# Cross products of one expert with kept first halves and early hub products, and a shared expert block's output products spread over six units

## The chip, the cores and the metric

The kernel runs on one core of one Trainium2 chip. The time is device microseconds of one execution. Before the change it is 2487.79 us, the median of 3 runs (2487.12 to 2488.73).

The core has a matrix engine (PE), two elementwise engines (DVE and POOL), an engine for activations and copies (ACT), and a queue that issues transfers (SP). Each works through its own list of instructions in order and waits for the others by semaphores.

## The reference

A gated layer with 8 weighted experts and one shared expert, added to its input. In float32, for 8 sequences of 512 tokens of width 256, with 1024 hidden features per expert:

```python
g = einsum('bsd,edf->ebsf', h, Wg)
u = einsum('bsd,edf->ebsf', h, Wu)
expert_outs = einsum('ebsf,efd->ebsd', silu(g) * u, Wd)
expert_output = einsum('be,ebsd->bsd', gating_probs, expert_outs)
shared = einsum('bsf,fd->bsd', silu(h @ Sg) * (h @ Su), Sd)
return x + (1 - sg) * expert_output + sg * shared
```

## The kernel before

**Units.** The work is cut into units: 2 groups of 4 sequences, times 9 experts (the shared one is the ninth), times 2 groups of 4 blocks of 128 features. A unit takes 4 blocks of weights and 4 sequences, and makes the 16 gate and 16 up products of blocks with sequences. The width of 256 is two halves of 128.

**Fewer products.** Block i and sequence i are given a small constant each. The four products of equal index, the *hub*, are made in two halves: P_i from the first half (`P_step`, L697) and then Q_i on top (`Q_step`, L724). The twelve others come in six pairs (i, j): one product of differences (`R1_step`, L785), started from the seed f = P_j - P_i, serves both (i, j) and (j, i). Each of these then gets one product more (`R_step`, L802) and a correction by the hub results D. Thus a pair costs 3 products in place of 4, for gate and for up.

**Banks.** The results lie in PSUM banks: three for gate, three for up, and two (`po0`, `po1`) for the output products. A seed is copied into a bank by ACT (L784), DVE opens the second bank of the pair (L798) and adds D (L811), ACT takes silu (L681), DVE multiplies (L686). POOL makes weight operands u and wb (L606, L622, L623) and the sums `rows` and `cols` of the features (L848).

**Output products.** `down` makes 26 products of a unit with Wd, again in pairs (r, S or s, r) and with the sums (p with `rows`, q with `cols`). They begin in the second half of their unit, 15 of them there and 11 in the next, mixed into the gate and up products.

**One expert in eight blocks.** Expert 7 is handled with all 8 blocks and all 8 sequences at once. Its units have kinds. A (unit 14) makes blocks 0 to 3 with sequences 0 to 3. X (unit 15) makes the 16 cross pairs (i, n), i below 4, n from 4 to 7, with four more hub products n (`hub_P`, `hub_Q`). Z (unit 33) makes blocks 4 to 7 with sequences 4 to 7. L (unit 32) has only output products, since X left its features in DRAM; they run as a *guest*, in the last unit before Z and in Z itself (`guest_down`).

**Seeds of X.** For pair (i, n) the difference P_n - P_i is taken by `hub_difference` (L775): for gate on DVE, for up on POOL. P_i is loaded from DRAM for each pair anew (`load_P`), into the tile that then takes the difference.

**What sets the order.** Strings of letters: G takes the next step of gate and up, D the next output product, E the next step of the guest. PE and POOL follow the written order; DVE and ACT are ordered by the framework's scheduler, but for operations that are pinned. With each D from the second on, `step_ahead` also takes one step of making operands for later units: transposed inputs, and for each pair a difference, a scaling and two sums, which go to DRAM (`xs`, `xsX`, `xsZ`) and come back when wanted.

Of the kernel before, what the change touches and what calls it, by code (L numbers as in the profile page):

```python
# [16 lines left out]
def kernel(  # L17
# [52 lines left out]
    CO = tuple(c - 0.5 for c in CI)  # L70
    ACROSS = [(i, NI + j) for j in range(NI) for i in range(NI)]
# [232 lines left out]
    def prepare(h):  # L304

        for p, (i, j) in enumerate(PAIRS):
# [10 lines left out]
            gp.tensor_tensor(v, v, at[j][:, 0], ALU.subtract)  # L317
            yield
            if d != 1.0:
                gp.tensor_scalar(v, v, 1.0 / d, 0.0, ALU.mult, ALU.add)  # L320
                yield
            gp.tensor_tensor(B_j, v, B_j, ALU.add)
# [12 lines left out]
    def prepare_across():  # L335

        for q, (i, n) in enumerate(ACROSS):
            to = dram.tile([P, 3, S], F32, tag=f"xsX_{q}", name=f"xsX_{q}")
            if i == 0:
# [5 lines left out]
            f = form_tile()  # L345
            pin(ve.tensor_sub(f[:, 0], xhub[0, i][:, 0], hub[:, 0]))
            yield
            pin(ve.tensor_scalar(
                f[:, 0], f[:, 0], 1.0 / (CI[i] - CO[n - NI]), 0.0, ALU.mult, ALU.add
            ))  # L350
            yield
            yield
            pin(ve.tensor_add(f[:, 1], f[:, 0], hub[:, 1]))
            yield
# [12 lines left out]
    def prepare_inner():  # L367

        for p, (i, j) in enumerate(PAIRS):
# [12 lines left out]
            if d != 1.0:  # L382
                pin(ve.tensor_scalar(v, v, 1.0 / d, 0.0, ALU.mult, ALU.add))
                yield
# [133 lines left out]
    for h in range(NH):  # L518
        for e in range(NE):
            for g in range(GRP):  # L520
# [16 lines left out]
                u.ca, u.opened, u.xo, u.a2 = {}, {}, {}, None  # L537
# [3 lines left out]
    for u in units:  # L541
        u.nxt = next((v for v in units[u.n + 1 :] if v.kind != "L"), None)
        u.guest = units[u.n + 1] if u.nxt and u.nxt.kind == "Z" else None
        if u.kind != "N":
            u.oct = octets.setdefault(u.e, {})

# [34 lines left out]
    def make_at(u, i):  # L581
# [5 lines left out]
        if u.C[i] % 1.0 and i not in u.ca:  # L587
            scaled_w(u, i)
# [152 lines left out]
    def hub_P(u, n, m):  # L741

        bank = u.bank[n, n, m] = new_bank(u, m, f"c{n}{n}")
        nc.tensor.matmul(bank, u.raw[n][:, m, 0], u.xo[n][:, 0], start=True, stop=True)
        t = u.Ps[n, m] = zpool.tile([P, S], F32, tag="z", name=f"P{n}{m}_{u.name}")
        nc.scalar.copy(t, bank)
        store_half(u, ("P", n), m, t)

# [17 lines left out]
    def load_P(u, p):  # L766

        for m in range(2):
            t = ppool.tile([P, S], F32, tag="p", name=f"f{p}{m}_{u.name}")
            nc.sync.dma_start(t, u.oct["P", u.pairs[p][0]][:, m])  # L770
            u.f[p, m] = t

    def hub_difference(u, p, m):

        (gp if m else ve).tensor_tensor(  # L775
            u.f[p, m], u.Ps[u.pairs[p][1], m], u.f[p, m], ALU.subtract
        )
# [101 lines left out]

    def load_kept(u, what, pool, tag):  # L880
# [4 lines left out]
    def look_ahead(u, items):  # L885

        if u.kind not in "XL":
            return
        for k, what in enumerate(items):
            if isinstance(what, str):  # L890
                which = "rows" if what[0] == "p" else "cols"
                n, sums = int(what[1]), getattr(u, which)
                if u.kind == "L" and n not in sums:
                    sums[n] = load_kept(u, (which, n), sumpool, "sum")
                continue
            for i, j in (PAIRS[what], PAIRS[what][::-1]):
                if u.kind == "L" and (i, j) not in u.h_:
                    u.h_[i, j] = load_kept(u, ("h", i, NI + j), hpool, "h")
            if k < (2 if u.kind == "X" else 1) and what not in u.X:
# [3 lines left out]
    def down(u, acc):  # L903
# [102 lines left out]
        if u.kind == "X":  # L1006
            order = DOWN_ACROSS
        elif u.n + 1 < len(units):
# [4 lines left out]
        for k, what in enumerate(order):  # L1013
            look_ahead(u, order[k : k + 3])
            if isinstance(what, int):
                yield from pair(what)
# [177 lines left out]
    def prepare_next(u, p):  # L1194

        nxt = u.nxt
        if nxt.kind == "X":
# [15 lines left out]
            if p >= 4:  # L1213
                load_P(nxt, p - 4)
# [7 lines left out]
        if p == 4 and nxt.guest:  # L1222
            load_d(nxt.guest, iopool, "io")

    def end_next(u, p):

        nxt = u.nxt
        if nxt.kind == "X":
# [3 lines left out]
            if p == 5:  # L1232
                for m in range(2):
                    hub_difference(nxt, 0, m)
                seed(nxt, 0)
                for m in range(2):
                    hub_difference(nxt, 1, m)

    def first_step(u, m):

        nxt = u.nxt
        if nxt.kind == "X":
            hub_P(nxt, NI, m)
        elif nxt.kind == "Z":
# [10 lines left out]
    FORMS_AT = {6: 0, 7: 1, 8: 3, 9: 2, 10: 4, 13: 5}  # L1255

    def across(u):
# [5 lines left out]
        last = len(u.pairs) - 1  # L1263
        for q, (i, n) in enumerate(u.pairs):
            if i == 0:
                for m in range(2):
                    hub_Q(u, n, m)
                    yield
                    R1_step(u, q, m)
                    yield  # L1270
            if i == 0 and n + 1 < 2 * NI:
# [3 lines left out]
            if q + 2 <= last:  # L1275
                load_P(u, q + 2)
            if i == 1 and n + 1 < 2 * NI:
                hub_load(u, n + 1)
            if i == 3 and n + 2 < 2 * NI:
                load_w(u, n + 2)  # L1280
            if q >= last - 3:
                prepare_next(u, q - last + 5)
            if q < last and i < NI - 1:
# [5 lines left out]
            for m in range(2):  # L1289
                if i < NI - 1:  # L1290
                    R1_step(u, q + 1, m)
                    yield
                elif q < last:
                    hub_P(u, n + 1, m)
# [3 lines left out]
                for r in range(2):  # L1298
                    if (m, r) == COMBINE_AT and q < last:
                        w_combined(u, q + 1)  # L1300
                    R_step(u, q, m, r)
                    if q == last and m == 1 and r == 1:
                        last_scaled(u)
                    if m == 1 and r == 1:
                        h_sums(u, q)
                        if i == NI - 1 and q < last:
                            for k in range(2):
                                hub_difference(u, q + 1, k)
# [392 lines left out]
```

## Time and profile before

| what | value |
|---|---|
| median of 3 runs | 2487.79 us |
| the profiled execution, its own time | 2489.11 us |
| its span on the core | 2487.3 us |
| PE busy | 2444.6 us (98%), 5681 records |
| DVE, ACT, POOL busy | 81%, 51%, 86% of the span |
| mean granted PE clock | 0.995 |

A product of 128x128 by 128x512 in float32 shows as two records. The records overlap, so a record's mean time is longer than its share of PE. The span runs from the first to the last instruction; some 1.8 us of the execution lie outside it. X is near 1010 to 1150 us of the span, Z near 2250 to 2330 us.

### The profile page before, as it was taken

The numbers are of one execution on the slowest core, as the hardware profiler recorded it, in microseconds if no ns is written. First come the engines' busy times: TensorE is split into PE (matmuls) and PEld (weight loads), VectorE is DVE, ScalarE is ACT, GpSimd is POOL, SyncE is SP. The second block draws the span as 40 slices with busy tenths as digits, with TensorE's granted clock in tenths as the row PEclk, the third lists the DMA queues.
The fourth block names the chain that finished last, engine by engine and source line by source line (L and its number), as shares of the span: only waits on it lengthen the run. The fifth ranks groups of instructions, "written<-read, shape, count | busy, mean of one in ns | idle before, by whom it ended". The sixth has DMA issues, their size and how long they took to land.

```text
span 2487.3 us, 23311 instructions
## 1 busy us (share of the span) xinstructions
PE 2444.6 (98%) x5681; PEld 1071.0 (43%) x5681; DVE 2020.0 (81%) x2953; ACT 1280.3 (51%) x2400; POOL 2136.5 (86%) x2286
## 2 busy tenths in 40 slices
PE   9999999999999999999999999999999999999899
PEld 4444444444444444434444444444444444443344
DVE  8778888888888688877876888888888887777588
ACT  5545555555555555555455455555555555554443
POOL 8978899988899998887899988888888988887595
PEclk9999999999999999999999999999999999999999
DMA  5345333434444445685555454344443453364133
GB/s 176 104 107 168 119 118 115 133 125 136 135 141 154 154 156 191 219 285 164 165 199 195 164 166 161 94 110 119 110 115 106 123 140 102 104 200 148 46 107 76
DMA packets 271157, 351.25 MB, mean 141 GB/s; under 512 B 76720, under 2 KB 167344, under 8 KB 271024
## 3 DMA queue, kind: packets, MB, share of 16 engines
q1 hardware_dynamic: 268336, 349.12, 45.1%
q8 instruction: 47, 0.77, 0.1%
q10 hardware_dynamic: 2688, 0.66, 0.1%
q14 instruction: 86, 0.70, 0.1%
HBM read 293.08 MB, written 56.62 MB: 141 GB/s over the span
## 4 chain that ended last, share of the span: by engine, by line
PE 82%; POOL 9%; DVE 4%; issue 2%; DMA 2%; ACT 1%; SPq 0%; DVEq 0%; POOLq 0%; ACTq 0%
PE c L806 26%; PE c L789 13%; PE c L728 8%; PE c L700 8%; PE r L954 6%; PE r L994 6%; PE b L938 5%; PE S L938 4%; PE q L954 4%; POOL cols L848 2%; PE s L954 2%; POOL rows L848 2%; POOL wb L623 1%; POOL f L775 1%; POOL wb L622 1%
## 5 line engine op out<-in xcount | busy, mean ns | idle before, releaser
L806 PE MATMUL c<-b,wb 128*128 128x512 f32 x1760 | 865.2, 593 | 3.6 <-POOL rows L848 1.4
L681 ACT ACTIVATE sg<-c 128x512 f32<-128x512 f32 x576 | 343.6, 597 | 583.2 <-DVE c L811 323.6
L686 DVE SCALAR_TENSOR_TENSOR h<-sg,coef,c 128x512 f32<-128x512 f32 x576 | 427.2, 742 | 200.9 <-PE c L806 165.7
L806 PEld LDWEIGHTS c<-b,wb 128*128 128x128 f32 x1760 | 334.4, 190 | 428.0 <-issue 395.2
L789 PE MATMUL c<-v,u 128*128 128x512 f32 x880 | 456.4, 601 | 9.7 <-ACT c L784 9.2
L798 DVE TENSOR_TENSOR c<-D,c 128x512 f32<-128x512 f32 x440 | 303.6, 691 | 82.6 <-ACT sg L681 61.3
L848 POOL TENSOR_TENSOR cols<-cols,h 128x512 f32<-128x512 f32 x274 | 361.8, 1320 | 8.6 <-DVE h L686 8.6
L848 POOL TENSOR_TENSOR rows<-rows,h 128x512 f32<-128x512 f32 x274 | 359.9, 1314 | 6.7 <-DVE h L686 6.6
L811 DVE TENSOR_TENSOR c<-c,D 128x512 f32<-128x512 f32 x440 | 303.8, 690 | 32.4 <-PE c L806 31.8
L789 PEld LDWEIGHTS c<-v,u 128*128 128x128 f32 x880 | 163.9, 191 | 234.9 <-issue 152.5
L728 PE MATMUL c<-x,w 128*128 128x512 f32 x528 | 257.1, 598 | 3.9 <-DVE f L723 2.6
L700 PE MATMUL c<-x,w 128*128 128x512 f32 x524 | 251.9, 592 | 0.0
L606 POOL TENSOR_TENSOR u<-w,w 128x256 f32<-128x256 f32 x220 | 179.8, 818 | 68.8 <-PE c L789 66.0
L848 POOL TENSOR_TENSOR rows<-h,h 128x512 f32<-128x512 f32 x140 | 186.2, 1330 | 59.8 <-DVE h L686 50.2
L819 DVE TENSOR_TENSOR X<-h,h 128x512 f32<-128x512 f32 x213 | 227.8, 1070 | 6.5 <-DMA h<-oct_h 1.1
L848 POOL TENSOR_TENSOR cols<-h,h 128x512 f32<-128x512 f32 x140 | 207.3, 1480 | 14.6 <-PE b L938 13.4
L954 PE MATMUL r<-h,wd 128*128 128x512 f32 x426 | 219.2, 596 | 0.0
L994 PE MATMUL r<-X,ud 128*128 128x512 f32 x426 | 218.3, 594 | 0.0
L739 ACT COPY D<-c 128x512 f32<-128x512 f32 x261 | 152.0, 585 | 89.3 <-DVE h L686 89.1
L706 ACT COPY P<-c 128x512 f32<-128x512 f32 x198 | 115.4, 587 | 110.0 <-PE c L700 105.8
L784 ACT COPY c<-f 128x512 f32<-128x512 f32 x242 | 143.6, 594 | 36.1 <-DVE h L686 14.1
L938 PE MATMUL b<-rows,wd 128*128 128x512 f32 x288 | 149.3, 600 | 12.5 <-ACT b L937 8.6
(152 smaller groups left out, 3391.0 us busy)
## 6 DMA issues: line engine op xcount, KB each, us to landing
b<-xs SPq DMA_DIRECT2D x192, 512.0 KB, 3.8
v<-xs SPq DMA_DIRECT2D x192, 256.0 KB, 2.8
wd<-in_L_cond_Wd_dram SPq DMA_DIRECT2D x32, 512.0 KB, 5.0
w<-in_L_cond_Wu_dram SPq DMA_DIRECT2D x124, 128.0 KB, 3.8
w<-in_L_cond_Wg_dram SPq DMA_DIRECT2D x123, 128.0 KB, 3.7
xsX<-form SPq DMA_DIRECT2D x48, 256.0 KB, 2.9
form<-xo SPq DMA_DIRECT2D x16, 512.0 KB, 4.5
f<-oct_P SPq DMA_DIRECT2D x32, 256.0 KB, 4.3
```

The costliest lines, as they stand in the source:

```text
L681: nc.scalar.activation(s, bank, AF.Silu)
L686: ve.scalar_tensor_tensor(t, u.sg[i, j], coef[:, u.e, b : b + 1], bank, ALU.mult, ALU.mult)
L700: nc.tensor.matmul(bank, u.raw[i][:, m, 0], xhub[u.h, i][:, 0], start=True, stop=True)
L728: nc.tensor.matmul(bank, u.at[i][:, m], xhub[u.h, i][:, 1], start=False, stop=True, skip_group_check=True,)
L789: nc.tensor.matmul(bank, u.U[p][:, m], u.V[p], start=False, stop=True, skip_group_check=True)
L798: made = ve.tensor_sub(other, u.Ds[j, m], u.bank[j, i, m])
L806: nc.tensor.matmul(bank, u.W[p][:, r, m], u.VB[p][:, r], start=False, stop=True, skip_group_check=True,)
L811: ve.tensor_add(bank, bank, u.Ds[j, m])
L848: gp.tensor_tensor(sums[n], other, u.h_[at], ALU.add)
L938: nc.tensor.matmul(po, w, b, start=not full, stop=True, skip_group_check=full)
L954: nc.tensor.matmul(po, w, b, start=True, stop=True)
L994: nc.tensor.matmul(A, u.Ud[p], u.X[p], start=False, stop=True, skip_group_check=True)
```

## The change

The number of products is the same. Five things differ.

1. **P_i stays.** The four tiles P_i are loaded once, in unit A, into the four places of the inputs x, which are written to DRAM beforehand and loaded again at the end of X. `hub_difference` is gone; `hub_f` makes all 32 differences on DVE: 28 of them take P_n straight from its bank, the four of the first hub with i = 2 and 3 from the copied tile.
2. **Hub products early.** `hub_P` and `hub_Q` for the next n go into `po0` and `po1`, at pairs 1, 2 and 3 of the four pairs before. Each pair takes its reversed product (r = 1) first. The string of X leaves the two banks free of output products meanwhile.
3. **Guest over six units.** L's 26 output products run in units 26 to 31, four or five each (E), between the two parts of the unit's own. Their sums and features are loaded at letters L, some steps earlier. Z has none.
4. **Making operands.** In the tables for later units, scalings go to ACT, and a difference and a sum of `prepare` go from POOL to DVE. `step_ahead` runs with D number 1, 2 and 9 to 25, not 2 to 25.
5. The strings after X and Z, and where forms of Wd are made, are written anew.

On POOL, in X, around the operands of pairs 5 to 7. Before (u, wb: weight operands of a pair; rows, cols: sums; f: the seed for up):

```order
L622 TENSOR_TENSOR wb0_7_1_5_7887<-u0_7_1_5_7784,wb0_7_1_5_7887 128x256
L623 TENSOR_TENSOR wb0_7_1_5_7887<-wb0_7_1_5_7887,u0_7_1_5_7784 128x256
L775 TENSOR_TENSOR f61_0_7_1_7923<-P51_0_7_1_7865,f61_0_7_1_7923 128x512
L848 TENSOR_TENSOR cols0_0_7_1_7961<-h40_0_7_1_7716,h50_0_7_1_7952 128x512
L606 TENSOR_TENSOR u0_7_1_8_7965<-w0_7_0_0_6883,w0_7_1_6_7845 128x256
L622 TENSOR_TENSOR wb0_7_1_6_7958<-u0_7_1_6_7839,wb0_7_1_6_7958 128x256
L623 TENSOR_TENSOR wb0_7_1_6_7958<-wb0_7_1_6_7958,u0_7_1_6_7839 128x256
L775 TENSOR_TENSOR f71_0_7_1_7969<-P51_0_7_1_7865,f71_0_7_1_7969 128x512
```

Now:

```order
L628 TENSOR_TENSOR wb0_7_1_5_7905<-u0_7_1_5_7790,wb0_7_1_5_7905 128x256
L629 TENSOR_TENSOR wb0_7_1_5_7905<-wb0_7_1_5_7905,u0_7_1_5_7790 128x256
L860 TENSOR_TENSOR cols0_0_7_1_7937<-h40_0_7_1_7690,h50_0_7_1_7922 128x512
L596 TENSOR_TENSOR w0_7_1_6_7714<-at0_7_1_6_7939,w0_7_1_6_7714 128x2x128
L612 TENSOR_TENSOR u0_7_1_8_7944<-w0_7_0_0_6857,w0_7_1_6_7714 128x256
L628 TENSOR_TENSOR wb0_7_1_6_7956<-u0_7_1_6_7844,wb0_7_1_6_7956 128x256
L629 TENSOR_TENSOR wb0_7_1_6_7956<-wb0_7_1_6_7956,u0_7_1_6_7844 128x256
```

One f per pair is gone from POOL's list. On DVE, in X, the same stretch now holds the differences of hub 6 (f80 to f110: seeds of its pairs, for gate; f81 and on: for up; h: features):

```order
L767 TENSOR_TENSOR f80_0_7_1_7974<-c660_0_7_1_7968,P0_0_7_1_7307 128x512
L767 TENSOR_TENSOR f90_0_7_1_7976<-c660_0_7_1_7968,P1_0_7_1_7371 128x512
L767 TENSOR_TENSOR f100_0_7_1_7978<-c660_0_7_1_7968,P2_0_7_1_7429 128x512
L823 TENSOR_TENSOR c511_0_7_1_7896<-c511_0_7_1_7896,D11_0_7_0_7174 128x512
L692 SCALAR_TENSOR_TENSOR h51_0_7_1_7985<-sg51_0_7_1_7961,coef_119,c511_0_7_1_7896 128x512
L692 SCALAR_TENSOR_TENSOR h15_0_7_1_7988<-sg15_0_7_1_7966,coef_119,c151_0_7_1_7918 128x512
L810 TENSOR_TENSOR c251_0_7_1_7981<-D51_0_7_1_7866,c521_0_7_1_7951 128x512
L767 TENSOR_TENSOR f81_0_7_1_7999<-c661_0_7_1_7994,P0_0_7_1_7307 128x512
L767 TENSOR_TENSOR f91_0_7_1_8001<-c661_0_7_1_7994,P1_0_7_1_7371 128x512
L767 TENSOR_TENSOR f101_0_7_1_8003<-c661_0_7_1_7994,P2_0_7_1_7429 128x512
L823 TENSOR_TENSOR c520_0_7_1_7949<-c520_0_7_1_7949,D20_0_7_0_7184 128x512
L767 TENSOR_TENSOR f110_0_7_1_8032<-c660_0_7_1_7968,P3_0_7_1_7489 128x512
```

Twelve DVE instructions stand from f80 to f110; PE has ten products between the P product of bank c660, which f80 reads, and the Q product onto it, which must follow f110. On PE, at the end of Z, before (B, b: the guest's products with its sums; c: gate and up):

```order
L938 MATMUL B1_1_7_0_16877<-cols_11_7_0_16777,wd1_7_0_15801 128x512
L806 MATMUL c320_1_7_1_16809<-b1_7_1_5_16789,wb1_7_1_5_16791 128x512
L938 MATMUL S3_1_7_1_16884<-h21_1_7_1_16785,wd1_7_1_3_16802 128x512
L938 MATMUL b1_1_7_0_16890<-rows_11_7_0_16836,wd1_7_0_15801 128x512
L806 MATMUL c230_1_7_1_16804<-b1_7_1_5_16789,wb1_7_1_5_16791 128x512
L994 MATMUL r3_1_7_1_16872<-X3_1_7_1_16787,ud1_7_1_3_16800 128x512
L938 MATMUL B2_1_7_0_16903<-cols_21_7_0_16875,wd1_7_0_15801 128x512
```

Now the guest's first products stand in unit 26, with gate and up products of that unit between them:

```order
L958 MATMUL b0_1_7_0_13686<-rows_01_7_0_13557,wd1_7_0_13354 128x512
L818 MATMUL c020_1_4_0_13636<-b1_4_0_1_13465,wb1_4_0_1_13453 128x512
L958 MATMUL B0_1_7_0_13693<-cols_01_7_0_13559,wd1_7_0_13354 128x512
L818 MATMUL c200_1_4_0_13631<-b1_4_0_1_13465,wb1_4_0_1_13453 128x512
L801 MATMUL c031_1_4_0_13680<-v1_4_0_2_13467,u1_4_0_2_13457 128x512
L974 MATMUL r0_1_7_0_13710<-h_1_41_7_0_13596,wd1_7_0_0_13602 128x512
```

The core of the diff:

```diff
+    SEATS = 6
...
-            gp.tensor_tensor(v, v, at[j][:, 0], ALU.subtract)
+            pin(ve.tensor_sub(v, v, at[j][:, 0]))
...
-                gp.tensor_scalar(v, v, 1.0 / d, 0.0, ALU.mult, ALU.add)
+                pin(nc.scalar.mul(v, v, 1.0 / d))
...
-            gp.tensor_tensor(B_j, v, B_j, ALU.add)
+            pin(ve.tensor_add(B_j, v, B_j))
...
-            pin(ve.tensor_scalar(
-                f[:, 0], f[:, 0], 1.0 / (CI[i] - CO[n - NI]), 0.0, ALU.mult, ALU.add
-            ))
+            pin(nc.scalar.mul(f[:, 0], f[:, 0], 1.0 / (CI[i] - CO[n - NI])))
...
+    for z in units:
+        if z.kind == "Z":
+            for k in range(SEATS):
+                host = units[z.n - 1 - SEATS + k]
+                host.guest, host.seat = units[z.n - 1], k
...
-        bank = u.bank[n, n, m] = new_bank(u, m, f"c{n}{n}")
+        if n == NI:
+            bank = new_bank(u, m, f"c{n}{n}")
+        else:
+            turned[m] = False
+            bank = ps_o.tile([P, S], F32, tag=f"po{m}", name=f"c{n}{n}{m}_{u.name}")
+        u.bank[n, n, m] = bank
...
+    def hub_f(u, n, i, m):
+        q = NI * (n - NI) + i
+        pool, tag = (zpool, "z") if i == 2 else (ppool, "p")
+        t = u.f[q, m] = pool.tile([P, S], F32, tag=tag, name=f"f{q}{m}_{u.name}")
+        at = u.Ps[n, m] if n == NI and i > 1 else u.bank[n, n, m]
+        ve.tensor_sub(t, at, u.P_[i][:, m])
...
-    def hub_difference(u, p, m):
-        (gp if m else ve).tensor_tensor(
-            u.f[p, m], u.Ps[u.pairs[p][1], m], u.f[p, m], ALU.subtract
-        )
+    def load_P(u, i):
+        u.P_[i] = xpool.tile([P, 2, S], F32, tag="x", name=f"P{i}_{u.name}")
+        nc.sync.dma_start(u.P_[i], u.oct["P", i])
...
+    GUEST_LOADS = (
+        ("p0", "q0"), (0,), ("p1",), (1,), ("q1", "p2"), (2,), ("q2",), (3,), ("p3",), (4,), ("q3",), (5,),
+    )
...
-                for r in range(2):
+                for r in (1, 0):
...
+                if more and (i, m) in HUBS_AT:
+                    make, k = HUBS_AT[i, m]
+                    make(u, n + 1, k)
+                    for k_ in (0, 1, 2) if make is hub_P else ():
+                        hub_f(u, n + 1, k_, k)
+                    yield
+                if more and (i, m) == (2, 0):
+                    for k_ in range(2):
+                        hub_f(u, n + 1, 3, k_)
+
+    HUBS_AT = {
+        (1, 0): (hub_P, 0), (1, 1): (hub_P, 1), (2, 1): (hub_Q, 0), (3, 0): (hub_Q, 1),
+    }
...
-        "Z": "GDGD" + "GEGEGE" + "GDGDGD" + "GEGDD" * 3
-        + "GDGDGDGEGEGE" + "GDGDGDGEGEG" + "GDGDGDGEGEGE" + "GDEGDEGDEGEGEGE",
+        "Z": 'GGGDGGDGGDGGDGGDGGDGDGGDGGDGGDGGDGGDGGDGDGGDGGDGGDGGDGDGD',
...
-    AHEAD_AT = range(2, 26) if OCT else (8, 11, 14, 17, 20)
+    AHEAD_AT = (1, 2, *range(9, 26)) if OCT else (8, 11, 14, 17, 20)
```

More of the change, by code (lines that the diff above doesn't have):

```diff
@@ L885, in look_ahead @@
     def look_ahead(u, items):
-        if u.kind not in "XL":
+        if u.kind != "X":
             return
         for k, what in enumerate(items):
[L890 to L899, printed above, removed]
+            if isinstance(what, int) and k < 2 and what not in u.X:
                 if k == 0 or PAIRS[what] in u.h_ and PAIRS[what][::-1] in u.h_:
@@ L1007, in down @@
             order = DOWN_ACROSS
+        elif u.kind == "L":
+            order = DOWN_GUEST
         elif u.n + 1 < len(units):
@@ L1015, in down @@
             if isinstance(what, int):
+                if u.kind == "L":
+                    h_difference(u, what)
+                    yield
                 yield from pair(what)
@@ L1221, in prepare_next @@
             load_d(nxt)
-        if p == 4 and nxt.guest:
+        if p == 4 and nxt.seat == 0:
             load_d(nxt.guest, iopool, "io")
@@ L1263, in across @@
         last = len(u.pairs) - 1
-        for q, (i, n) in enumerate(u.pairs):
[L1265 to L1271, printed above, removed]
+        for m in range(2):
+            hub_Q(u, NI, m)
+            yield
+            R1_step(u, 0, m)
+            yield
+        for q, (i, n) in enumerate(u.pairs):
+            more = n + 1 < 2 * NI
+            if i == 1 and more:
                 make_at(u, n + 1)
@@ L1403, in gate_up @@
                 d_forms(u, step - 11)
-            if step in (3, 5, 7, 9, 11) and u.n > 1 and nxt is not None and not u.guest:
+            if step in ((3, 5, 7, 9) if u.guest else (3, 5, 7, 9, 11)) and u.n > 1 and nxt is not None:
                 d_forms(u, (step - 3) // 2)
@@ L1421, in gate_up @@
                 prepare_next(u, p)
[L1422 to L1426 removed]
+                if u.kind == "Z":
+                    for k in {3: (0,), 4: (1,), 5: (2, 3)}.get(p, ()):
+                        d_forms(u, k)
+                elif u.guest and p in (2, 3):
+                    d_forms(u, p + 2)
                 elif p == 2 and u.n:
@@ L1575 @@
         elif u.guest:
-            order = ORDERS["host"]
+            order = ORDERS["host", u.seat]
         elif prior.kind in "XZ":
-            order = ORDERS["after"]
+            order = ORDERS["after", prior.kind]
         else:
             order = ORDER
-        take = TAKES.get(u.kind, TAKE)
+        take = TAKES.get(u.kind, 28 if prior and prior.kind == "Z" else TAKE)
         chores, nC = {}, 0
@@ L1645 @@
                     next(visiting)
+                    continue
+                if what == "L":
+                    if u.seat == 0 and not u.guest.ad:
+                        make_ad(u.guest)
+                    next(arriving)
                     continue
```

121 lines of the change are left out of this document (56 added, 65 removed).

## The prediction

> **What bounds the kernel now.** I read the page's first part, then the table by stretches, then PE's waits, then the chain in the bad stretches.
>
> ```profile
> PE 2444.6 (98%) x5681; PEld 1071.0 (43%) x5681; DVE 2020.0 (81%) x2953; ACT 1280.3 (51%) x2400; POOL 2136.5 (86%) x2286
> ```
>
> PE is busy nearly always, but records overlap, so 98% does not say that nothing is to be had. The table by stretches does, since it counts records (busy us, and xcount, for PE, PEld, DVE, ACT, POOL; then granted clock, DMA share, GB/s):
>
> ```profile
> 140.00:160.00 20.00, 17.35 (x37) 7.22 (x36) 14.81 (x25) 8.91 (x17) 16.56 (x20) 0.91 0.20 46
> 200.00:600.00 400.00, 399.86 (x928) 175.03 (x927) 347.70 (x510) 210.31 (x394) 361.91 (x380) 1.00 0.42 130
> 825.00:860.00 35.00, 32.23 (x69) 13.80 (x68) 22.30 (x33) 15.59 (x31) 32.23 (x36) 0.90 0.45 151
> 1010.00:1150.00 140.00, 130.68 (x289) 53.84 (x288) 104.15 (x148) 73.23 (x144) 114.48 (x119) 0.98 0.75 243
> 2215.00:2360.00 145.00, 127.52 (x283) 53.28 (x282) 95.70 (x139) 63.60 (x117) 105.62 (x123) 0.98 0.38 120
> ```
>
> The second row is ordinary units: 400 us for 928 records, 0.431 us each, 0.862 us a product. At this pace the other rows would take 15.9, 29.7, 124.6 and 122.0 us. They lose 4.1, 5.3, 15.4 and 23.0 us: 47.8 us in all, and that is about what any reordering can win, as the number of products stays.
>
> PE's own waits name the causes:
>
> ```profile
> PE c L789 <- ACT c L784: 9.2, 12, 2.8
> PE b L938 <- ACT b L937: 8.6, 6, 3.6
> PE b L938 <- DMA rows<-oct_rows: 3.8, 2, 2.0
> PE q L954 <- POOL cols L848: 3.3, 2, 2.8
> PE B L938 <- DMA cols<-oct_cols: 3.0, 2, 1.9
> PE c L728 <- DVE f L723: 2.6, 1, 2.6
> ```
>
> The first row is X: PE waits for a seed copy. What is late before the copy stands in X's groups on POOL and DVE (busy, mean; then idle and its releaser) and in the chain:
>
> ```profile
> L775 POOL TENSOR_TENSOR f<-P,f 128x512 f32<-128x512 f32 x16 | 21.0, 1325 | 3.5 <-ACT P L746 3.5
> L775 DVE TENSOR_TENSOR f<-P,f 128x512 f32<-128x512 f32 x16 | 15.3, 972 | 1.5 <-DMA f<-oct_P 1.3 <-ACT P L746 0.2
> ...
> 1054.91 3.48 issue
> 1058.42 2.50 POOL f L775 x2
> ```
>
> The up seeds' differences are on POOL, between sums and weight operands, and POOL hands on late. The second row is mostly, the third and fifth are wholly the guest's. At Z's end loads and products alternate:
>
> ```profile
> 2314.43 2.64 DMA cols<-oct_cols
> 2317.21 1.11 PE B L938 x2
> 2318.33 2.56 DMA rows<-oct_rows
> ...
> 2321.03 1.11 PE b L938 x2
> ```
>
> The load waits for a free `sum` tile, so it starts when the product before it is done.
>
> The 2.8 us for `cols` is at 835 us. There POOL makes operands ahead in the middle of its sums:
>
> ```profile
> 830.82 1.23 POOL form L322
> 832.05 1.23 POOL rows L848
> 833.28 0.42 POOL ud L661
> ...
> 834.49 1.23 POOL cols L848
> ```
>
> The 2.6 us for f is at 147 us, where DVE took h (and two accumulations) first:
>
> ```profile
> 144.71 0.75 DVE h L686
> ...
> 146.76 2.41 DVE f L723 x4
> ```
>
> **A wait costs more than itself.** Clock after the wait at 835 us:
>
> ```profile
> 835.76 2.08 PE L954 MATMUL q<-cols,wd 128*128 128x512 f32 x2 [2.77 <-POOL cols L848]
> ...
> 835.00:842.00 7.00, 6.24 (x8) 2.62 (x9) 0.77 (x2) 0.72 (x2) 6.84 (x9) 0.51 0.59 204
> ```
>
> After 2.77 us idle PE ran 7 us at half clock, so the loss is 5.3 us. [...]
>
> **The change, part by part, against the profiled execution's 2489.1 us.**
>
> *X.* POOL loses 16 differences: 114.48 - 21.0 = 93.5 us. DVE gives up its 16 (15.3 us) and gets 32: 28 with one operand in a bank, which I price by the first row below at 0.687, and four from tiles at 0.972.
>
> ```profile
> L721 DVE TENSOR_TENSOR f<-P,c 128x512 f32<-128x512 f32 x66 | 44.7, 687 | 39.7 <-ACT P L706 38.6
> L798 DVE TENSOR_TENSOR c<-D,c 128x512 f32<-128x512 f32 x440 | 303.6, 691 | 82.6 <-ACT sg L681 61.3
> L686 DVE SCALAR_TENSOR_TENSOR h<-sg,coef,c 128x512 f32<-128x512 f32 x576 | 427.2, 742 | 200.9 <-PE c L806 165.7
> ```
>
> DVE comes to 104.15 - 15.3 + 28 x 0.687 + 4 x 0.972 = 112.0 us, PE to 124.6 us, so PE is the longest again. But DVE's work comes in bursts: of the twelve instructions from f80 to f110, seven differences, three of the kind of L798 and two of L686 are 8.4 us, and PE has ten products, 8.6 us, before the Q product that waits for f110. With no slack, and behind a DVE at 90%, I charge 1 us for each of three such hubs and 1 us for the first: 4 us. Bounds: 0, if DVE always runs ahead; 15 us, if each of the 16 pairs still waits about as now. Transfers ease: 32 loads of 256 KB become four of 512 KB. X: 15.4 to 4, **-11.4 us**.
>
> *Z and its neighbours.* The guest's products leave. No PE time is saved: 26 x 0.862 = 22.4 us moves to units 26 to 31. The 23.0 us lost go, but for a late start of Z's own operands and for POOL, which has the 24 sums of a unit in a shorter Z: I leave 5 us (bounds 2 and 12; the chain shows 1 to 2 us of POOL after Z even now). **-18 us**.
>
> *The six hosts.* The loads stand at the 8th and 12th step, the first guest product after the 22nd: at least ten products, 8.6 us, against landings of 2.6 us. Sums and features of a guest take one or two tiles of the unit's own; the transfers held behind such a load on SP are wanted a dozen products later. What remains is the copy into and out of the bank for products with sums, where ordinary units show no wait. I charge 0.5 us a unit: **+3 us** (bounds 0 and 32: every unit waiting once as at 835 us).
>
> *Operands off the slab.*
>
> ```profile
> L317 POOL TENSOR_TENSOR form<-form 128x512 f32<-128x512 f32 x6 | 8.1, 1350 | 3.6 <-DMA form<-xd 3.6
> L322 POOL TENSOR_TENSOR form<-form 128x512 f32<-128x512 f32 x6 | 7.6, 1272 | 0.1
> L320 POOL TENSOR_SCALAR form<-form 128x512 f32<-128x512 f32 x3 | 1.9, 620 | 0.1
> L348 DVE TENSOR_SCALAR form<-form 128x512 f32<-128x512 f32 x16 | 10.9, 679 | 0.0
> L353 DVE TENSOR_TENSOR form<-form 128x512 f32<-128x512 f32 x16 | 17.8, 1115 | 0.0
> L383 DVE TENSOR_SCALAR form<-form 128x512 f32<-128x512 f32 x3 | 1.8, 605 | 0.0
> ```
>
> POOL gives up 8.1 + 7.6 + 1.9 = 17.6 us. DVE takes 12 at up to 1.115 = 13.4 us and gives up 10.9 + 1.8 = 12.7 us, so it stays even. ACT takes 22 scalings, which I price at 0.6 us by those DVE rows: 13 us, hidden as ACT is 51% busy. At 835 us L322 is one of those that leave; I take back 4.8 of 5.3 us (bounds 0 and 5.3). At 147 us no operand is made in the slab any more, and the changed DVE order has f020 to f121 ahead of h11 in that unit: 4 of 4.1 us. Later operands finish about three units later and the closing sums of the first sequences fall into the hosts; DVE is busier there, +1 us. **-7.8 us**.
>
> Sum: -11.4 - 18 + 3 - 7.8 = -34.2 us, so 2455 us for the profiled execution, and 1.3 us less against the median: 2453.6. One more row is short of the pace, the stretch after X:
>
> ```profile
> 1150.00:1480.00 330.00, 326.94 (x760) 143.57 (x759) 256.91 (x380) 172.28 (x321) 297.20 (x318) 1.00 0.50 168
> ```
>
> 760 x 0.431 = 327.6, so 2.4 us are lost there, with POOL at 90%. The strings after X are new, and X hands over less POOL work; I take 1.6 us of it. **I forecast 2452 us.**
>
> **Rivals.**
>
> *X stays as it is, bound by DVE.* The second order in the diff says why it could: 8.4 us of DVE in 8.6 us. Against it: 112.0 against 124.6 us over the whole stretch. Price: X's 11.4 us not won: 2463 us.
>
> *The hosts wait.* Guest and unit share accumulators and the two banks, and such a product waited 3.6 us at worst before. Six units with one wait and its half clock, 6 x 5.3 = 32 us in place of 3: 2481 us. Against it: ordinary units have eight products with sums each too, and in the row of 400 us PE idles 0.14 us in all.
>
> *Slower: ACT held by pinned scalings.* Each of the 22 is pinned in ACT's order one step after a DVE difference that waits for a landing, and behind it in ACT's order stand seeds and silu, for which PE waits. From 36 us / 22 = 1.6 us of PE wait each, nothing is won; at 2.2 us each (12 us more): 2500 us. Against it: these differences were pinned on DVE before, in the same steps, and units with them kept the pace.
>
> *The change does nothing for Z,* because the loads merely wait elsewhere: then 18 us less is won, 2470 us.
>
> **How the numbers follow.** Forecast 0.66, its own range 2440 to 2462 (X and Z at their low bounds give 2445, hosts at theirs 2442, and a little for the stretch after X; X and Z some 5 us worse each give 2462). X bound by DVE 0.14, Z unmoved 0.05, hosts wait 0.10, ACT 0.05. The range 2437 to 2474 holds the first three, but for some 0.04 of their own tails, and leaves out hosts and ACT: 0.8. A measurement of this kernel tells some 0.2%, 5 us, from no change. The first three and nearly all of the hosts' case lie over 5 us below 2487.8: faster 0.90; same 0.05, from the hosts' and ACT's cases; slower 0.05, ACT's.
>
> **What would show it.** In the profile after: X's row with some 289 records in about 128 us and POOL near 94, DVE near 112; no wait of PE on oct_rows or oct_cols; PE's wait L789 <- ACT seed down to 2 to 4 us; no half clock near 147 and 835 us; hosts at about 83 products x 0.862 = 71.5 us each. The forecast is wrong if PE waits for L767 or for the seeds behind it by more than 8 us in X, if a half clock stands in units 26 to 31, or if ACT rows of the operands show as releasers of PE's seeds.

## The result and the profile after

The changed kernel takes 2443.46 us (median of 4 runs, 2443.06 to 2446.69), the kernel before 2487.45 us beside it. The ratio is 0.9826, 95% interval 0.9809 to 0.9843: 44 us, or 1.7%, are won. The forecast was 2452 us with the range 2437 to 2474, so the sign held and, in the main, the mechanism, and the gain was 8.5 us larger than said. The profiled execution took 2446.69 us, the slowest of the four; its span is 2444.9 us.

The first part of its page, and the table by stretches (columns as in the prediction: length, busy time and records of PE, PEld, DVE, ACT and POOL, then granted clock, DMA share and GB/s):

```profile
PE 2428.9 (99%) x5681; PEld 1070.9 (44%) x5681; DVE 2030.8 (83%) x2962; ACT 1290.2 (53%) x2422; POOL 2098.4 (86%) x2255
```

```profile
140.00:160.00 20.00, 20.00 (x48) 8.87 (x47) 16.58 (x27) 11.77 (x22) 16.56 (x20) 1.00 0.13 27
200.00:600.00 400.00, 399.55 (x930) 175.88 (x929) 336.56 (x496) 216.78 (x405) 349.27 (x370) 1.00 0.43 134
825.00:860.00 35.00, 34.89 (x82) 15.05 (x81) 28.05 (x40) 19.63 (x38) 28.55 (x31) 1.00 0.61 198
1002.00:1128.00 126.00, 125.14 (x289) 53.95 (x288) 107.19 (x164) 73.23 (x147) 91.04 (x101) 1.00 0.72 236
1150.00:1480.00 330.00, 326.65 (x756) 143.25 (x755) 257.38 (x375) 171.82 (x321) 291.50 (x310) 0.99 0.51 164
1803.00:2157.00 354.00, 353.76 (x824) 156.18 (x823) 306.33 (x438) 188.96 (x352) 299.96 (x323) 1.00 0.43 123
2235.00:2278.00 43.00, 42.02 (x98) 18.26 (x97) 34.95 (x52) 20.28 (x38) 40.44 (x45) 1.00 0.65 190
```

The fourth row is X: the 289 records that took 140 us now take 126 us, with DVE at 107 and POOL at 91 us. The sixth is the first five of the six hosts and the last is Z: both at 0.43 to 0.44 us a record, which is the pace of the ordinary row (400 / 930 = 0.430). The rows at 147 and 835 us run at full clock. Only the fifth row is no better than before (0.437 us a record, 0.434 before). PE's longest waits (who waited for what: us in all, times, the longest):

```profile
PE c L818 <- DMA b<-xs: 2.9, 2, 2.2
PE c L801 <- ACT c L796: 2.1, 8, 0.4
PE c L818 <- POOL wb L628: 1.8, 3, 1.0
PE c L801 <- POOL ud L667: 1.5, 2, 1.0
```

All six rows of waits quoted before are gone or below 1 us, but for the seed copy (now L796), which fell from 9.2 us to 2.1. A new one leads: b, an operand of the gate and up products that comes from the tables. Other signs that the prediction listed came too: POOL near 94 us and DVE near 112 us in X (91 and 107), no wait on `oct_rows` or `oct_cols`, no half clock at 147 and 835 us or in units 26 to 31.

To set this beside the prediction's terms, I cut PE's instructions into units (from a unit's first gate or up product to the next unit's) and took off 0.8584 us for each product, its spacing in undisturbed stretches. What is left is the unit's loss, in us, in the two profiled executions:

| place | before | after | difference | forecast |
|---|---|---|---|---|
| X | 16.7 | 2.1 | -14.6 | -11.4 |
| Z, the unit before (the sixth host) and the one after | 24.4 | 2.2 | -22.2 | -18 |
| units 26 to 30 (hosts) | 1.3 | 0.8 | -0.5 | +3 |
| unit with the wait at 147 us | 5.5 | 0.7 | -4.8 | -4 |
| unit with the wait at 835 us | 6.1 | 0.6 | -5.5 | -4.8 |
| other units ahead of X | 4.7 | 3.2 | -1.5 | |
| four units after X | 4.1 | 2.5 | -1.6 | -1.6 |
| units 20 to 25 | 2.6 | 8.6 | +6.0 | +1 |
| last unit | | | +1.9 | 0 |

(The rows add up to -42.8 us; the 0.4 us to the -42.4 us between the two spans is rounding.)

Units 20 to 25 lose where they did not lose before. The largest piece is in unit 21: 2.2 us of wait for b, and 1.7 us because the clock is halved (0.50) for 3.4 us behind it. A second wait for b in unit 22 (0.7 us) and one for POOL in unit 24 (1.0 us) follow; the other 3 us lie in smaller places. The chain of waits at the largest (start, duration, what):

```profile
1455.76 0.87 PE c L801 x2
1457.04 5.95 DMA b<-xs
1463.13 1.38 PE c L818 x2
```

SP's list at that place says why b's load went out late (start, duration, line, operation; SPq is SP's queue):

```profile
1448.78 0.46 SPq L570 DMA_DIRECT2D w<-in_L_cond_Wu_dram  x1
1455.16 0.34 SPq L415 DMA_DIRECT2D oct_cols<-form  x1
1455.55 0.92 SPq L404 DMA_DIRECT2D form<-oct_h  x2
1456.57 0.38 SPq L450 DMA_DIRECT2D v<-xs  x1
1457.04 0.38 SPq L488 DMA_DIRECT2D b<-xs  x1
```

For 5.8 us SP stands at the store of a sum that POOL has not yet made (`SPq L415 <- POOL form L412` in SP's own waits); the loads of v and b for PE stand behind it. So b's load goes out 13.3 us after the one before it, where 7.7 us is usual within a unit, and it lands after 5.95 us, where the median is 3.8. These sums of X's kept features are made by the same steps as the tables. With fewer steps per unit they run later than before, into units in which they meet other work; that the place of the steps has to do with this loss is borne out by a run below (u3). Such a hold is not always costly: the kernel before has one of 7.0 us at a store of this kind, and in all of these units PE waits 0.5 us for b.

### The profile page after: what moved, and what is told of

Its sections match the earlier page's. It is cut to its first block, busy times and chain, and to the rows that moved or that the text cites. A ratio compares the mean times of both kernels' runs of the same rounds, so it can differ in the third digit from the quotient of the medians.

```text
span 2444.9 us, 23271 instructions
## 1 busy us (share of the span) xinstructions
PE 2428.9 (99%) x5681; PEld 1070.9 (44%) x5681; DVE 2030.8 (83%) x2962; ACT 1290.2 (53%) x2422; POOL 2098.4 (86%) x2255
## 4 chain that ended last, share of the span: by engine, by line
PE 89%; DVE 6%; POOL 2%; issue 1%; ACT 1%; DMA 1%; SPq 0%; DVEq 0%; ACTq 0%; POOLq 0%
PE c L818 27%; PE c L801 14%; PE c L734 9%; PE c L706 9%; PE r L974 7%; PE r L1014 6%; PE b L958 5%; PE q L974 5%; PE S L958 5%; PE s L974 2%; DVE h L692 1%; DVE c L823 1%; DVE f L767 1%; POOL rows L860 1%; DVE c L810 1%
## 5 line engine op out<-in xcount | busy, mean ns | idle before, releaser
L823 DVE TENSOR_TENSOR c<-c,D 128x512 f32<-128x512 f32 x440 | 303.5, 690 | 23.2 <-PE c L818 22.2
L860 POOL TENSOR_TENSOR cols<-h,h 128x512 f32<-128x512 f32 x140 | 200.4, 1431 | 0.2 <-DVE h L692 0.2
L796 ACT COPY c<-f 128x512 f32<-128x512 f32 x242 | 143.5, 595 | 32.1 <-DVE h L692 23.2
L734 PEld LDWEIGHTS c<-x,w 128*128 128x128 f32 x528 | 99.9, 190 | 127.3 <-issue 98.3
```

Source lines behind the costliest of these rows:

```text
L734: nc.tensor.matmul(bank, u.at[i][:, m], xhub[u.h, i][:, 1], start=False, stop=True, skip_group_check=True,)
L823: ve.tensor_add(bank, bank, u.Ds[j, m])
L860: gp.tensor_tensor(sums[n], other, u.h_[at], ALU.add)
```

## The experiments

The kernel before took 2485.9 to 2487.8 us beside these runs. Losses and gains below are differences to 2443.46 us, good to some 2 us.

**One part undone at a time.** The first four runs each undo one of the change's parts. X as before:

```diff
-                for r in (1, 0):
+                for r in range(2):
...
-                if more and (i, m) in HUBS_AT:
-                    make, k = HUBS_AT[i, m]
-                    make(u, n + 1, k)
-                    for k_ in (0, 1, 2) if make is hub_P else ():
-                        hub_f(u, n + 1, k_, k)
-                    yield
...
+                        if i != NI - 2 and q + 2 <= last:
+                            for k in range(2):
+                                hub_difference(u, q + 2, k)
```

> The changed kernel with its cross unit put back: P_i loaded for each pair, the up differences on POOL, hub products in the gate and up banks at the start of each row of pairs, the old strings of X and of the unit after. Guest and operand parts stay changed. Theory: the parts hardly touch each other, and X's loss goes from 2.1 back to about 16.7 us: about 2443.5 + 16 = 2459 us, with POOL near 114 us in X's stretch. Rival (the gain in X came from operands no longer made just before it, in units 12 to 14): X loses 5 us or less, 2446 us.

Measured 2458.95 us (2458.33 to 2459.40), ratio to before 0.9886 [0.9871, 0.9901]. X's gain is 15.5 us, as the theory had it, X loses 17.6 us again, and both old rows are back: the wait for the seed and POOL's differences.

```profile
PE c L792 <- ACT c L787: 11.1, 15, 2.8
```

```profile
L778 POOL TENSOR_TENSOR f<-P,f 128x512 f32<-128x512 f32 x16 | 20.6, 1296 | 2.3 <-ACT P L749 2.3
```

The guest's products back in Z and the unit before:

```diff
-        u.guest, u.seat = None, None
+        u.guest = units[u.n + 1] if u.nxt and u.nxt.kind == "Z" else None
...
-                host.guest, host.seat = units[z.n - 1], k
...
+        "Z": "GDGD" + "GEGEGE" + "GDGDGD" + "GEGDD" * 3
+        + "GDGDGDGEGEGE" + "GDGDGDGEGEG" + "GDGDGDGEGEGE" + "GDEGDEGDEGEGEGE",
```

> The changed kernel with the guest put back into the last unit before Z and into Z, with the old strings there. Theory: Z, the unit before and the unit after lose some 21 us more again, with PE waiting for oct_rows and oct_cols: about 2465 us. Rival (part of the loss near Z came from sums on POOL and goes with the other parts): 2455 us or less.

Measured 2469.00 us (2468.22 to 2469.81), 0.9927 [0.9912, 0.9941]: this part is worth 25.5 us, more than the 21 us of the theory. Z and its neighbours lose 28.5 us, and PE waits on the guest's operands as it did before the change:

```profile
PE b L944 <- ACT b L943: 6.5, 5, 3.0
PE b L944 <- DMA rows<-oct_rows: 6.2, 2, 4.3
PE B L944 <- DMA cols<-oct_cols: 2.4, 2, 1.3
```

The steps of operand making back on the slab, then the engines back while the steps stay off it:

```diff
-    AHEAD_AT = (1, 2, *range(9, 26)) if OCT else (8, 11, 14, 17, 20)
+    AHEAD_AT = range(2, 26) if OCT else (8, 11, 14, 17, 20)
```

> The changed kernel with operand steps at output products 2 to 25 again, not at 1, 2 and 9 to 25; which engine makes them stays changed. Theory: the wait at 147 us comes from these steps (4.8 us), the one at 835 us from POOL's share of the operands: 2443.5 + 5 = 2448 us, 147 us back and 835 us clean. Rival: both waits come from steps in the hub: 2453 us.

```diff
-            pin(ve.tensor_sub(v, v, at[j][:, 0]))
+            gp.tensor_tensor(v, v, at[j][:, 0], ALU.subtract)
...
-                pin(nc.scalar.mul(v, v, 1.0 / d))
+                gp.tensor_scalar(v, v, 1.0 / d, 0.0, ALU.mult, ALU.add)
...
-            pin(ve.tensor_add(B_j, v, B_j))
+            gp.tensor_tensor(B_j, v, B_j, ALU.add)
...
-            pin(nc.scalar.mul(f[:, 0], f[:, 0], 1.0 / (CI[i] - CO[n - NI])))
+            pin(ve.tensor_scalar(
+                f[:, 0], f[:, 0], 1.0 / (CI[i] - CO[n - NI]), 0.0, ALU.mult, ALU.add
+            ))
```

> The changed kernel with the operand differences, sums and scalings back on POOL and DVE, but the steps still outside the hub. Theory: POOL in the middle of its sums is what made PE wait at 835 us, so a wait of that kind comes back in one of the units where these tables are made: about 2449 us. Rival: the place of the steps is all that matters: 2443.5 us, no change.

Steps on the slab: 2447.28 us (2445.53 to 2449.46), 0.9840 [0.9825, 0.9854]. The wait at 147 us is back, and the one at 835 us is not, as the theory had it:

```profile
PE c L734 <- DVE f L729: 2.6, 1, 2.6
```

Engines back: 2444.11 us (2442.95 to 2444.55), 0.9825 [0.9809, 0.9841], which can't be told from the full change: the rival's value, not the theory's. At 835 us PE still keeps the pace:

```profile
825.00:860.00 35.00, 34.88 (x82) 15.16 (x81) 28.54 (x41) 18.34 (x35) 29.05 (x31) 1.00 0.44 136
```

So the wait at 835 us goes with either edit alone, the one at 147 us with the steps alone, and moving operations to ACT and DVE gained nothing that the steps had not gained already. The 3.8 us of the steps are a balance: with them on the slab the unit at 147 us loses 4.9 us more and the other units ahead of X 6.4 us more (9.6 in place of 3.2), but units 20 to 25 lose 2.2 us in place of 8.6, and PE waits for b only 0.7 us in the whole run. With the engines back those units lose 3.7 us. By these single profiles the later place of the steps and the engines both have a share in that loss. The four parts undone one by one cost 15.5, 25.5, 3.8 and 0.7 us, 45.5 in all, beside the 44.0 won: they hardly depend on each other.

**X: engine or place?** The change takes differences off POOL and also makes them earlier. Here they stay early, and half of them go to POOL, which takes P_n from the copied tile in place of the bank:

```diff
-        at = u.Ps[n, m] if n == NI and i > 1 else u.bank[n, n, m]
-        ve.tensor_sub(t, at, u.P_[i][:, m])
+        at = u.Ps[n, m] if m or n == NI and i > 1 else u.bank[n, n, m]
+        (gp if m else ve).tensor_tensor(t, at, u.P_[i][:, m], ALU.subtract)
```

> The changed kernel, but in X the 16 hub differences of the second half (m = 1) are made by POOL, from the pair's resident P, where DVE made them; their place, two pairs ahead in the down banks, stays. POOL's busy time in X goes up by 16 x 1.3 = 21 us, DVE's down by 11. Theory: what made X wait was POOL between its sums and weight operands, so the wait comes back wherever POOL makes seeds: most of the 14.6 us that X won is lost again, 2455 to 2460 us. Rival: it was the place of the differences, made only just before their seeds; with them two pairs ahead it does not matter which engine makes them, so X loses at most 3 us more than now, 2443 to 2447 us.

Measured 2453.87 us (2452.93 to 2456.82), 0.9873 [0.9858, 0.9887]: 10.4 us lost, just under the theory's 2455 to 2460 us and far from the rival's. X's loss goes from 2.1 to 11.6 us. But the waits are others than the theory's. Of this run, PE's two longest rows, and one place of the chain:

```profile
PE c L818 <- POOL wb L629: 6.9, 3, 3.8
PE s L974 <- DVE accB L941: 2.0, 1, 2.0
```

```profile
1063.69 3.73 POOL f L767 x3
1067.42 1.23 POOL rows L860
```

In X PE no longer waits for a seed: made early, and with P_i in place, the differences have time. POOL makes them three in a row, 3.73 us, and what is late now is the weight operand wb behind them. So both halves of the change in X matter: the early place, together with the P_i that stay, removed the wait for seeds even with POOL making half of them, and DVE took over the load that otherwise hits the weight operands. Whether differences on DVE in the old, late place would have done as well no run shows.

**X: has DVE slack?** The prediction said no, and charged 4 us. Two runs add DVE work of known size, by making differences twice, of half the hubs (w1) and of all (v2):

```diff
+        if m:
+            ve.tensor_sub(t, at, u.P_[i][:, m])
         ve.tensor_sub(t, at, u.P_[i][:, m])
```

```diff
+        if True:
+            ve.tensor_sub(t, at, u.P_[i][:, m])
         ve.tensor_sub(t, at, u.P_[i][:, m])
```

> The changed kernel, but in X DVE makes every hub difference twice, one after the other: 28 x 0.687 + 4 x 0.972 = 23 us more of DVE in X, about 135 us in all against PE's 120. Theory of the prediction, that DVE has no slack there at the bursts: X is at least the 14 us longer by which DVE exceeds PE, and the bursts add to it, 2460 to 2467 us. Rival: DVE's work for X can begin in the unit before and end in the one after, so that X gets only a part of the 23 us: 2445 to 2452 us.

> The changed kernel, but in X DVE makes the 16 hub differences of m = 1 twice: 11 us more of DVE, 103.2 + 11 = 114 us in the 120 us of X, so still less than PE. Making all 32 twice (23 us more) made X 24.1 us longer. Theory, DVE has no slack in X's bursts: about all 11 us show, 2452 to 2456 us. Rival, it is DVE's total alone, and 24.1 us came of 126 us of DVE with other waits behind: 0 to 4 us, 2443 to 2448 us.

All twice: 2468.81 us (2467.90 to 2469.41), 0.9931 [0.9914, 0.9947]. Half: 2452.74 us (2452.35 to 2453.61), 0.9864 [0.9849, 0.9879]. X of each, in the table by stretches (half, then all):

```profile
1001.90:1130.40 128.50, 120.50 (x278) 51.46 (x277) 114.08 (x174) 71.15 (x141) 87.41 (x98) 1.00 0.67 221
```

```profile
1002.00:1146.60 144.60, 127.67 (x278) 53.79 (x277) 125.96 (x190) 70.58 (x141) 88.18 (x98) 0.95 0.61 198
```

11.4 us added (16 more instructions of 0.71) made X 7.9 us longer and the kernel 9.3; 23.1 us added made X 24.1 us longer and the kernel 25.4. In the first case DVE is busy for 114 of 128.5 us, so its total does not bind: PE waits for the f of a burst, and once for an accumulation behind it.

```profile
PE c L774 <- DVE f L769: 4.4, 3, 1.5
PE q L976 <- DVE accV L945: 2.7, 1, 2.7
```

By this run DVE has some 3.5 us of slack in X (11.4 less 7.9), though in the 126 us of the changed kernel's row it is idle for 19. PE's waits in that row add up to 7.9 us, against 0.9 in the changed kernel's X, and the clock is not halved there (1.00); the kernel's 9.3 us are in the theory's range. Of the 23.1 us all show and a little more, but part of that is the clock: it is 0.95 on the mean above, by an estimate from that mean about four stretches of 3.4 us at half speed, up to 6.8 us. Without them 17.3 us are left, and the slack would be 5.8 us. It is small in both, 3.5 to 6 us, and the kernel's 25.4 us lie above the range that the theory gave.

**X: the order of r.** The turned order is in the list of changes, and the prediction gave it no price.

```diff
-                for r in (1, 0):
-                    if (m, r) == (0, 1) and 0 < q < last:
+                for r in (0, 1):
+                    if (m, r) == (0, 0) and 0 < q < last:
```

> The changed kernel, but in X the down products of a pair run in the order r = 0, 1, as they did before, where the change has 1, 0; the weight operands and sums keep their places between them. Theory: the order was turned so that the product that needs the operand made last comes last; turned back, PE waits for that operand in up to 16 places by some 0.3 us, 3 to 6 us, 2447 to 2450 us. Rival: operands are ready in time in either order, under 1.5 us, 2442 to 2445 us.

Measured 2449.33 us (2447.97 to 2450.63), 0.9850 [0.9835, 0.9865]: 5.9 us, as the theory's size. X loses 6.3 in place of 2.1 us. In the waits of X, though, stand seeds and sums, not weight operands:

```profile
PE c L801 <- ACT c L796: 2.2, 8, 0.3
PE q L974 <- POOL cols L860: 1.0, 1, 1.0
PE b L958 <- POOL cols L860: 0.4, 1, 0.4
```

So the size was right, and the reason only in part: the rows of waits account for 3.6 us, against 0.9 in the changed kernel's X, and no single operand is behind them.

**Hosts: does the lead of the loads matter?** In the six hosts both loads are put right ahead of the first guest product:

```diff
-        ("host", 0): 'GGDGGDGGDGGDLGGDGGDLGGDGGDGGDGGDGDGGEGEEGGEGEGGEGGDGDGGDGDGGDGDGGDGGDGDGGDGDGGDGDGGDGD',
+        ("host", 0): 'GGDGGDGGDGGDGGDGGDGGDGGDGGDGGDGDGGLLEGEEGGEGEGGEGGDGDGGDGDGGDGDGGDGGDGDGGDGDGGDGDGGDGD',
```

> The changed kernel, but in the six hosts both loads of the guest stand right ahead of the first guest product (as they stood in the unit before Z and in Z) and no longer ten or more products earlier. Theory: it is this lead that took away the waits on oct_rows and oct_cols, so each host waits some 2 us for its loads and then runs at half clock for some 3 us: 6 x 4 to 5 us = 24 to 30 us, 2468 to 2474 us. Rival: what counts is that a host has other products around the guest's, and a load that comes late is still covered as the first guest product needs one load alone: under 6 us, 2444 to 2450 us.

Measured 2459.80 us (2459.40 to 2462.14), 0.9896 [0.9882, 0.9911]: 16.3 us, between the two. The row that grew is a load of the guest, but it is of h, a feature tile, and oct_rows and oct_cols, the loads of sums, don't appear:

```profile
PE r L974 <- DMA h<-oct_h: 11.8, 5, 4.9
```

```profile
2126.18 4.69 DMA h<-oct_h
2131.01 1.19 PE r L974 x2
...
2200.77 6.46 DMA h<-oct_h
2207.36 2.04 PE r L974 x2
```

So the loads of h need the lead: they come two at a letter and landed 5.0 us after issue in the median (3.5 in the changed kernel, where nobody waits for them). Behind two of the waits the clock was halved: from 2086 to 2235 us it is 0.98 on the mean, by an estimate from that mean about two stretches of 3.4 us at half speed. The theory counted a wait and a half clock in each of six hosts; there were five waits and two halvings.

Of the loads of sums the run says nothing, as they did not move. In the program as built SP issued them where it did before, and only the loads of h went out late. In the first host:

```profile
1810.63 0.32 SPq L911 DMA_DIRECT2D rows<-oct_rows  x1
1836.75 0.90 SPq L911 DMA_DIRECT2D h<-oct_h  x2
```

In the changed kernel the two stand at 1813.66 and 1816.64 us. The first guest product runs at 1837.0 us, 26 us after the load of its sum, so what a late load of sums would cost in a host stays open.

**Three tries at a faster kernel.** The loss in units 20 to 25 led to three edits: a step at each of 2 to 25 after X only (v4), the stores of the sums two steps later, so that SP would not stand (w3), and that with the engines back (w4).

```diff
-                if u.n >= 2 and nD in AHEAD_AT and u.kind in "NA":
+                if u.n >= 2 and nD in (range(2, 26) if u.n > 15 else AHEAD_AT) and u.kind in "NA":
```

> The changed kernel with the steps that make operands kept off the slab up to X, and with a step at each of the places 2 to 25 after X (as before the change). Meant to be faster. Theory: units 21 to 24 lose 8 us in the profile of the changed kernel because the sums behind X are made late, at the same time as their tables; made sooner they lose some 2 us, and the wait at 147 us stays away: 2436 to 2440 us. Rival: the 8 us were mostly one half clock of that execution, and steps in the slab cost in these units what they cost in the first: 2442 to 2446 us.

Measured 2443.62 us (2441.91 to 2445.68), 0.9830 [0.9815, 0.9844]: no difference, as the rival had it. The loss of units 20 to 25 is 6.7 us in place of 8.6, and lies in other places of the same six units. The 1.9 us are mostly the half clock of the one profiled execution: without its 1.7 us the changed kernel's loss would be 6.9 us, and seven of the other kernels, with the operands made as in the changed one, lose 5.4 to 7.1 us there (u1, u2, v1, v2, v3, w1, w2).

```diff
                 gp.tensor_tensor(to, to, halves[1][:, 0], ALU.add)
                 yield
                 yield
+                yield
+                yield
```

> The changed kernel, but the store of each sum of kept features behind X is issued two steps later, when POOL has made the sum. In the profile of the changed kernel SP's queue stood 6.4 us at such a store, and a load of b behind it came late. Meant to be faster. Theory: that hold is what costs units 21 to 24 most of their 8 us: 2437 to 2441 us. Rival: the hold is one event, worth 2 us of wait and now and then a half clock, and later stores delay the tables further: 2442 to 2446 us.

> The changed kernel with both: operands made on POOL and DVE as before the change (their steps stay off the slab), and the later store. Meant to be faster. Theory: with the engines back alone 2444.1 us, units 21 to 24 lost 3.7 us in its profile in place of 8, so that the two together come to 2437 to 2441 us. Rival: what is left above the pace (about 15 us in some 30 places of 0.3 to 2 us) is not of these units, and nothing changes beyond 2442 to 2446 us.

Measured 2448.31 us (2448.06 to 2449.88), 0.9846 [0.9829, 0.9862], and 2456.15 us (2455.81 to 2457.58), 0.9878 [0.9864, 0.9893]: both slower than the changed kernel, which neither theory nor rival had. SP's own waits of the first between 1430 and 1460 us, and PE's:

```profile
SPq L417 <- POOL form L412: 12.5, 1, 12.5
```

```profile
PE c L820 <- DMA b<-xs: 4.0, 1, 4.0
```

At this place a longer hold of SP (12.5 in place of 5.8 us) came with a longer wait for b (4.0 in place of 2.2). But length alone does not decide: in v4 SP stood for 24.1 us at such a store, in u4 for 10.6, and no wait for b was over 1.6 us in either. What stands behind the hold, and how soon PE wants it, is the likelier measure, but no run isolates it. The remedy was wrong: every step behind the store moved too, and another store (of oct_rows, where it was oct_cols) met POOL at a worse place. With the engines back as well, b waits 3.4 us in another unit, and of the last two units a wait of 1.9 us for an operand of POOL's (`PE b L964 <- POOL ad L662`) is the longest; why those shifted is open. None of the kernels run beats the changed one.

## Why the prediction was right, and where it was off

- **What bounds it.** The reading that PE sets the pace everywhere and that some 47.8 us in four stretches is about all that reordering can win held as far as the runs go: 44 us were won, the stretches named are those that gained, and no run here won more.
- **X (-11.4; measured -14.6).** The sum's mechanism is borne out by three runs, with one correction: POOL's load in X does cost PE (v1), but through weight operands and not seeds once the differences are made early; and DVE has little slack (w1, v2). Mis-sized was the charge "4 us" for DVE's bursts: X's whole loss is 2.1 us. The turned order of r was listed with the change and not weighed: w2 puts 4.2 us of X on it, and without it X would lose 6.3 us, more than the 4 charged, and gain 10.4, a little less than forecast. What X won beyond the forecast thus came of a part that the sum did not weigh, which is luck.
- **Z (-18; measured -22.2).** "I leave 5 us" was too much: Z, with the unit before and after, loses 2.2. The lower bound, 2, was the better value. POOL was indeed full in Z (40.44 of 43 us in the last row of stretches), and still no PE wait of note came of it.
- **Hosts (+3; measured -0.5).** The charge of 0.5 us a unit was for copies into and out of the bank; the row of 1803 to 2157 us shows 824 records in 354 us, the ordinary pace. The reason given for no waits, ten products of lead, is shown by v3 for the loads of h: without it 16.3 us are lost. For the loads of sums no run shows it.
- **Operands (-7.8 in all).** The two waits went as said (-4.8 and -5.5). The reason "L322 is one of those that leave" is enough at 835 us (u3), but not needed: with L322's work still on POOL (u4), the place of the steps alone removes the wait too. The "+1 us" for later operands was the term most in error: +6.0 in units 20 to 25 of the profiled execution, 1.7 of it the half clock. I priced the later work by the engine that does it, DVE, and left out the queue it goes through: SP held at a store, with PE's loads behind, which with the half clock is 3.9 us of the 6.0. The rest is spread over smaller waits, and what moved them is open, beyond that the loss is 2.2 us with the steps on the slab (u3) and 3.7 us with the engines back (u4).
- **The rivals.** X bound by DVE did not come, but was close: w1 shows that 11 us more on DVE would have lost 9.3. Hosts waiting is ruled out by their pace. ACT held by pinned scalings is ruled out too: u4 takes the scalings off ACT, and the time stays.
- **The sum.** The terms gave -35.8 us, and profile against profile it is -42.4: X 3.2, Z 4.2 and hosts 3.5 better, operands 2.0 worse (-4.8 - 5.5 - 1.5 + 6.0 = -5.8 against -7.8), the last unit 1.9 worse. The other 1.9 us come from the profiled execution, which is 3.2 us over its median, where the one before was 1.3.

## What to carry to other kernels

When work leaves an engine that is late, ask for its place in the program and its engine separately: here the early place, with its inputs kept, cured one wait and the other engine a second. Average idle time says little of slack: DVE was idle for 19 us of X's row and could take some 3.5 to 6. And price a delayed store by what stands behind it on its queue, not by the engine that makes the data alone; the length of the hold did not tell the cost here, and moving the store "a little later" was no remedy, as the steps behind it moved too.

## What the runs showed of the hardware

**Waits and the halved clock.** The prediction said that a wait costs more than itself, by the one at 835 us. In these runs some waits were followed by half clock and some were not, and their length alone does not tell which. Two waits of the run with differences on POOL show it, of 2.12 and 3.79 us. Of the table by stretches, the 3.4 us that hold the shorter wait and the next 3.4 us, and then the 6.8 us that hold the longer one and the next 3.4 us (the third column is PE's busy time; the clock stands third from the end):

```profile
1069.20:1072.60 3.40, 1.28 (x4) 0.39 (x3) 0.86 (x2) 1.92 (x4) 3.40 (x5) 1.00 0.80 295
1072.60:1076.00 3.40, 3.40 (x6) 1.34 (x5) 1.39 (x2) 1.19 (x2) 3.32 (x5) 0.50 0.01 5
1099.90:1103.30 3.40, 1.50 (x4) 0.38 (x2) 1.71 (x3) 2.69 (x6) 3.32 (x5) 1.00 1.03 319
1103.30:1106.70 3.40, 1.51 (x4) 0.79 (x5) 0.35 (x1) 0.00 (x0) 3.40 (x5) 1.00 0.85 310
1106.70:1110.10 3.40, 3.40 (x10) 1.49 (x9) 2.11 (x4) 2.10 (x4) 3.40 (x4) 1.00 0.18 66
```

Behind the 2.12 us PE ran for 3.4 us at a clock of 0.50, and by an estimate from these two numbers the wait cost 2.12 + 1.7 us; behind the 3.79 us the clock was 1.00, and that wait cost only itself. PE was idle for 2.12 us of the 3.4 us ahead of the half clock, and for 1.90 and 1.89 us of the two stretches of 3.4 us that hold the longer wait.

The profiled executions of the kernel before and the changed one have seven half clocks ahead of their last 2 us: from 149.0, 835.1, 1091.1, 1125.2, 2261.8 and 2330.1 us on before, and from 1463.8 us on after. The one from 835.1 us on lasts 6.8 us, the others 3.4. In the 3.4 us right ahead of each PE was idle for 1.93 to 3.40 us. Of the kernel before, 3.4 us from 2323.3 us on with 1.60 us of idle were followed by 3.4 us at 1.00. What sets the two cases apart no run isolates.

In the changed kernel the wait for b, 2.22 us, was followed by 3.4 us at 0.50; in another kernel (w1) PE's longest wait for b was 2.2 us as well, and the mean clock of its profiled execution is 1.0. The other three executions of the changed kernel had a mean clock of 1.0 and spans of 2441.3 to 2442.0 us, so 1.7 of their 2.9 to 3.6 us below the profiled one are explained by the half clock; the rest is open.

**DVE beside POOL.** A difference of two tiles took DVE 1.089 us on the mean in the changed X, and 1.747 us in v1 (first row: changed kernel; second: v1). With one operand in a bank it took 0.68 us in both.

```profile
L767 DVE TENSOR_TENSOR f<-P,P 128x512 f32<-128x512 f32 x4 | 4.4, 1089 | 0.0
```

```profile
L767 DVE TENSOR_TENSOR f<-P,P 128x512 f32<-128x512 f32 x2 | 3.4, 1747 | 0.0
L767 DVE TENSOR_TENSOR f<-c,P 128x512 f32<-128x512 f32 x14 | 9.1, 683 | 2.4 <-ACT P L757 2.4
```

While both differences of v1 ran, POOL was making sums of 128x512 one behind the other. The run with all differences made twice (v2) has both cases: two differences beside such sums took 1.75 and 1.74 us, and two during which POOL was idle 0.68 and 0.69 us. A sum of POOL's took 1.71 us beside them; in the changed kernel one took 1.73 us beside differences of 1.37 and 1.16 us, and the sum before it 1.27. POOL's work at the same time does not settle it alone: the four differences of the changed kernel took 0.67, 1.15, 1.37 and 1.16 us, and POOL made a sum, of 1.81 us, beside the first of them too.

```profile
1022.03 3.42 DVE L769 TENSOR_TENSOR f<-P,P 128x512 f32<-128x512 f32 x2
1031.40 0.68 DVE L768 TENSOR_TENSOR f<-P,P 128x512 f32<-128x512 f32 x1
1023.19 1.71 POOL L862 TENSOR_TENSOR rows<-rows,h 128x512 f32<-128x512 f32 x1
```
